# Moving preparation into the first projection, and splitting a normalised map by a threshold on the raw one

## Chip, core and metric

The kernel runs on one core of one Trainium2 chip. The metric is the device time of the program in microseconds (us), the median of several runs. A profile is one more execution, taken by the hardware profiler.

The engines are named as in the profile: PE (TensorE, matmuls; PEld its weight loads), DVE (VectorE), ACT (ScalarE), POOL (GpSimd) and SP (SyncE). SP computes nothing here: it issues nearly all DMA transfers, in one queue, in order. A `q` behind an engine's name means its sequencer, which waits or issues.

## What is computed

The input `x` is four images of 96 channels, 128 x 128. Two layers follow, each a residual around a group norm (32 groups of three channels).

```python
x = x + ssm(_gn(x))       # 1x1 to 192 channels, depthwise 3x3, silu, four scans
                          # (rows, columns, both directions), layer norm, 1x1 back to 96
x = x + attn(_gn(x))
```

The second layer subtracts the mean of the whole image, and splits the result into its positive part `x1` and its negative part `x2`. Each is normalised with statistics of its own (numbers of positives and negatives, sums, sums of squares):

```python
x1 = relu(x); x2 = x - x1
out = 0.5 * (nc1 * x1n + nc2 * x2n) + res_coef * x   # xr
half1, half2 = sc1 * x1 + x1n, sc2 * x2 + x2n
key, qry = conv3x3(half1, aw1), conv3x3(half2, aw2)  # attention over channels and taps
value = conv3x3(half1, aw3)                          # convolved with the attention's weights
y2 = layer_norm(conv3x3(half2, w_conv2)) * half1
result = xr + conv1x1([layer_norm(attended), y2], w_full) + b_full
```

## The kernel before

**Stages.** `image_stats(0)` takes the group norm's statistics of image 0 (32 chunks of 96 x 512, one `bn_stats` each). `project(b)` makes the 192 channels of image b: 16 strips of eight rows, in each a load of the strip (`strip_in`), the norm on ACT (L454), seven shifted copies by DMA (L462, L467), 56 matmuls (L611) into three rotating PSUM banks, tanh on ACT (L486) and its product on DVE (L487), then the small projections for the scan (`rows_out`, `cols_out`) and stores. `ssm_scan` is one long generator over 384 steps; each has two halves with a scan on DVE (L831), softplus and exponential on ACT, and products on POOL and DVE. `norm` of an image is `ssm_output` (layer norm and the 1x1, into `xnew` in DRAM) and then `split_norm`. `direct_maps` makes keys, queries and attention weights of image 0; `attend` those of the other images and, for all, the attended map `od`; `close` (`attn_output`) is the last stage and writes the output.

**Order.** The generators are woven by hand. `co_run(left, right, pace)` draws `left`, and for each unit of its declared cost as much of `right` as `pace` says. From project 0 to the end of `direct_maps(0)`, `in_order` fixes the order of emission on every engine and on SP's queue: an instruction that waits holds all that is emitted behind it on that engine. Projects 0, 1 and 2 with 3 run beside the scan at paces 0.25, 0.75 and 1.35; the scan cannot begin before eight strips of project 0 are there, and needs all of it for its second direction. After that `norm(0)` runs beside the scan at 0.5, `direct_maps(0)` at 0.95. In the second part, `attend(b)` runs beside `close(b-1)` and `norm(b+1)`; `close(3)` runs alone at the end. There the order is left to the compiler's scheduler.

**What the change touches.**

- `image_stats(b + 1)` runs beside `project(b)`: a generator `beside`, drawn four times a strip (L623, L633), which loads a chunk of 192 KB (L401, one buffer) and takes its `bn_stats` (L404) one draw later. `project` then makes mean and variance with `bn_aggr` in `combine` (L181) and two small matmuls (L183, L190).
- Behind project 3 come `new_map` (borders of the six padded maps x1d, x2d, vd of two sets: twelve DMAs, L1175 and L1176) and `pair_weights` (3x3 weights of the attention: twelve loads into `g`, L1202; sums and differences of taps on DVE, L1185 to L1189; four stores `wd`, L1211; two passes over one buffer). Then `ssm_output` of image 0 loads `y` (L927) and sums it on PE (L938).
- `split_norm` has two passes over `xnew`, each of 16 chunks of 96 x 1024. The first takes counts and sums with `scale=a, bias=shift0` inside the Relu. The second first normalises the chunk in place on ACT (L1150), then makes for each half `scale * x + shift` on ACT (L1156), and masks it by the sign of the normalised chunk on DVE (L1161). Loads are L1041, stores L1165; a memset on POOL (L1154) clears the border column.
- `attn_output` does the same for its 16 chunks: it loads o, c2 and xx (L1718), normalises `xx` in place on ACT (L1727), makes x1 (ACT L1731, mask L1732), `c2 = (c2 - mean) * x1` (L1733), `e` (ACT L1737, mask L1738, L1739), two matmuls a half (L1743, L1744) and the sum (L1745); each tile has two buffers.

Of the kernel before, what the change touches and what calls it, by code (L numbers as in the profile page):

```python
# [9 lines left out]
F32 = mybir.dt.float32  # L10
# [7 lines left out]
C = 96  # L18
# [44 lines left out]
def kernel(  # L63
# [86 lines left out]
    ones = filled(1.0, "ones")  # L150
# [25 lines left out]
    def combine(ps, stats, mat, name):  # L176


        n = stats.shape[0]
        mv = small.tile([n, 2], F32, name=f"mv{n}", tag=f"mv{n}")  # L180
        nc.vector.bn_aggr(mv, stats)  # L181
        p1 = bank(ps)[:n, 0:2]
        nc.tensor.matmul(p1, lhsT=mat, rhs=mv, start=True, stop=True)  # L183
        r = small.tile([n, 2], F32, name=name, tag=name)
        nc.vector.tensor_copy(r, p1)
        d2 = small.tile([n, 1], F32, name=f"d2{n}", tag=f"d2{n}")
        nc.vector.tensor_sub(d2, mv[:, 0:1], r[:, 0:1])
        nc.vector.tensor_mul(d2, d2, d2)
        p2 = bank(ps)[:n, 0:2]
        nc.tensor.matmul(p2[:, 0:1], lhsT=mat, rhs=d2, start=True, stop=True)  # L190
        nc.vector.tensor_add(r[:, 1:2], r[:, 1:2], p2[:, 0:1])
        return r, mv
# [150 lines left out]
    def project_weights(pool):  # L343

        ws = []
        with tc.tile_pool(name="wq", bufs=1, side="left") as pq:
            for k, parts in enumerate(STACK):
                n = (128, 128, C + KK + 1)[k]  # L350
                m = 3 if k < 2 else 1
                w = pool.tile([n, m, 2 * C], F32, name=f"wp{k}")
                raw = pq.tile([n, 2 * C], F32, name=f"raw{k}")
                for p, c0, c1, dh, d in parts:
                    q = p + c1 - c0
                    nc.sync.dma_start(raw[p:q], in_wT[c0:c1])
                    src = dw_wT[3 * dh : 3 * dh + 3] if k < 2 else dw_wT[6 + d : 7 + d]
                    nc.sync.dma_start(w[p:q], src.partition_broadcast(q - p))
                if k == 2:
                    nc.sync.dma_start(raw[C : C + KK], in_b[0].partition_broadcast(KK))  # L360
                    nc.sync.dma_start(w[C : C + KK, 0], dw_wT)
                    nc.gpsimd.dma_start(
                        w[n - 1 : n, 0].rearrange("p (j c) -> p j c", j=2),
                        dw_b.rearrange("c j -> j c").unsqueeze(0),
                    )
                    nc.sync.dma_start(
                        raw[n - 1 : n].rearrange("p (j c) -> p j c", j=2),
                        ones[0:1].unsqueeze(1).to_broadcast([1, 2, C]),
                    )
                nc.vector.tensor_scalar(raw, raw, 0.5, None, ALU.mult)  # L370
                nc.vector.tensor_mul(w, w, raw.unsqueeze(1).to_broadcast([n, m, 2 * C]))
                ws.append(w)

            one = pq.tile([128, PW], F32, name="one")
            nc.vector.memset(one, 1.0)
            nc.vector.memset(one[:, 0:1], 0.0)
            where = dram.tile([1, (H + 2) * PW + 4], F32, name="where", bufs=1)
            nc.sync.dma_start(where[:, 0:PW], zeros[0:1, 0:PW])
            nc.sync.dma_start(
                where[0, PW : (H + 1) * PW].rearrange("(h w) -> h w", w=PW), one  # L380
            )
            nc.sync.dma_start(where[:, (H + 1) * PW :], zeros[0:1])
            taps = dram.tile([KK + 1, H * PW], F32, name="taps", bufs=1)
            for t in range(KK):
                at = (t // 3) * PW + t % 3
                nc.sync.dma_start(taps[t : t + 1], where[:, at : at + H * PW])
            nc.vector.memset(one, 1.0)
            nc.sync.dma_start(taps[KK].rearrange("(h w) -> h w", w=PW), one)
        return ws, taps

    def image_stats(b, pool):

        stats = pool.tile([C, NCH, 6], F32, name=f"stats{b % 2}", tag=f"stats{b % 2}")

        def run(p2, ahead):
            xf = x[b].rearrange("c h w -> c (h w)")
            tiles = []
            for i in range(NCH + ahead - 1):
# [6 lines left out]
                yield 0.7  # L405

        return stats, run

    def project(b, weights, stats, beside, zb, xrows, ps):
# [10 lines left out]
        with tc.tile_pool(name="a2", bufs=2, side="left") as p2:  # L420
            beside = beside(p2, 1) if beside else iter(())
# [20 lines left out]
            gs, _ = combine(ps, stats.rearrange("p c s -> p (c s)"), gmean, "gs")  # L442
# [155 lines left out]
            for s in range(last + 1):  # L598
# [3 lines left out]
                for q in range(3):  # L602
                    pz = bank(ps)
                    for i, (k, d) in enumerate(terms):
# [17 lines left out]
                        if i == 4:  # L622
                            next(beside, None)  # L623
# [4 lines left out]
                    if q == 1:  # L628
# [4 lines left out]
                        next(beside, None)  # L633
# [398 lines left out]
    def split_norm(xnew, x1d, x2d, stats, keep, cnt, ps, side):  # L1032


        with tc.tile_pool(name="n2", bufs=2, side=side) as p2:
# [10 lines left out]
            gs, mv = combine(ps, stats.rearrange("p c s -> p (c s)"), gmean, "gs1")  # L1046
            a = col("rstd1")
# [7 lines left out]
            shift0 = col("b1")  # L1055
# [35 lines left out]
            nc.tensor.matmul(pt, lhsT=ones, rhs=c5, start=True, stop=True)  # L1091
            g5 = col("g5", 5)
            nc.vector.tensor_copy(g5, pt)
# [34 lines left out]

            rs, rh, half = col("rs", 2), col("rh", 2), col("half", 2)
# [4 lines left out]


# [3 lines left out]
            ia = col("ia")  # L1139
            nc.vector.reciprocal(ia, a)  # L1140
            nc.vector.tensor_add(low[:, 0:1], rs[:, 1:2], ia)
            nc.vector.tensor_add(low[:, 1:2], rh[:, 1:2], bful)
            nc.vector.tensor_mul(ia, ia, shift0)
            nc.vector.tensor_sub(low[:, 1:2], low[:, 1:2], ia)
            keep.update(up=up, low=low, a=a, b=shift0, scale=scale, shift=shift)

            for i in range(NS):
                y = ahead.pop(0)
                piece(i + 3)
                nc.scalar.activation(y, y, AF.Identity, scale=a, bias=shift0)  # L1150
                v = y.rearrange("p (h w) -> p h w", w=W)
                for side_, m in ((0, x1d), (1, x2d)):
# [9 lines left out]
                        to, v, 0.0, to, op, ALU.mult  # L1162
# [28 lines left out]
    def pair_weights():  # L1191


        four, nine = [], []
        with tc.tile_pool(name="wq", bufs=1, side="left") as pw:
            for i, pair in enumerate(((aw1, aw3), (aw2, w_conv2))):
                g = pw.tile([C, 3, 3, 2, C], F32, name="g")
                for j, src in enumerate(pair):
                    v = src.rearrange("c (h w) o -> c h w o", w=3)
                    for w in range(3):  # L1200

                        nc.sync.dma_start(g[:, :, w, j], v[:, :, w if j else 2 - w])  # L1202
                g = g.rearrange("p h w j o -> p h w (j o)")
# [9 lines left out]
        return four, nine  # L1213
# [450 lines left out]
    def attn_output(img, ps, side):  # L1664
        keep = img.keep
        up, low, scale, shift = (keep[n] for n in ("up", "low", "scale", "shift"))
        ob = out[img.b].rearrange("c h w -> c (h w)")
        with (
# [54 lines left out]
            for t in range(NS):  # L1723
                o, c2, xx = ahead
                if t + 1 < NS:
                    ahead = loads(t + 1)
                nc.scalar.activation(  # L1727
                    xx, xx, AF.Identity, scale=keep["a"], bias=keep["b"]
                )
                x1 = p3.tile([C, SN], F32, name="x1")  # L1730
                nc.scalar.activation(x1, xx, AF.Identity, scale=scale[:, 0:1], bias=shift[:, 0:1])  # L1731
                nc.vector.scalar_tensor_tensor(x1, xx, 0.0, x1, ALU.is_gt, ALU.mult)  # L1732
# [5 lines left out]
                nc.vector.scalar_tensor_tensor(e, xx, 0.0, e, ALU.is_gt, ALU.mult)  # L1738
# [55 lines left out]
    def projections(images, weights, stats, wp, ps):  # L1794
        for b in images:
            beside = None
            if b + 1 < NB:
                stats[b + 1], beside = image_stats(b + 1, wp)
# [8 lines left out]
    with tc.tile_pool(name="wp", bufs=1, side="left") as wp:  # L1807
# [7 lines left out]
        for images, pace in (([0], 0.25), ([1], 0.75), ([2, 3], 1.35)):  # L1815
            left = projections(images, weights, stats, wp, psl)
            if images[0] == 0:
                next(left)
                next(others)
                while ready[0] < 2:  # L1820
                    next(left)
                wdt, wbc, outws, outbs = next(others)
            co_run(left, last, pace)
            drain(left)
    maps = [
        [new_map(f"{n}{i}") for n in ("x1d", "x2d", "vd")] for i in range(2)
    ]
    four, nine = pair_weights()
# [113 lines left out]
```

## Time and profile before

| | |
|---|---|
| Median of 3 runs (lowest, highest) | 6966.72 us (6951.81, 6972.1) |
| The profiled execution | 6980.28 us |
| Its span, first to last instruction | 6978.5 us |
| Mean granted TensorE clock | 0.888 |
| First matmuls of projects 0, 1, 2, 3 | 56.3, 440.3, 899.1, 1526.8 us |
| `ssm_output` of image 0, first matmul | 2165.6 us |
| Second pass of `split_norm`, image 0 | 2500.6 to 2603 us |
| Scan, first to last | 304.1 to 3395.8 us |
| Last close, first `bn_aggr` to the end | 6849.0 to 6978.5 us |

Times in the profile are microseconds from the span's start unless marked ns. A row of busy time by stretches gives each engine's busy time and, behind x, its instructions. A row of waits gives what waited for what: the sum in us, the number of times, the longest. A row of the timeline gives start, duration, engine, line, operation, names, and in brackets the engine's idle time before it with what ended it. "A<-B" reads: A is written from B. Matmul ends are modelled, so busy PE is not PE at its peak.

### The profile page before, as it was taken

To read this page: it belongs to the slowest core of one execution; us is meant where nothing else is said; L and a number is where in the kernel's file an instruction comes from. 1 tells how busy PE (TensorE), PEld (TensorE's weight loads), DVE (VectorE), ACT (ScalarE), POOL (GpSimd) and SP (SyncE) were. 2 spreads that over 40 slices of the span, in tenths; PEclk is the share of its full clock that TensorE was granted. 3 is DMA by queue.
4 is the path that set the end of the run, shared out by engine and by line. 5 is a ranking of instruction groups with operands and counts; after the bars stand their busy time and mean duration, and the time that the engine had idled before them with its cause. 6 is when DMAs were issued, how large, how long until landed. Compare 5 with 4: busy or idle time off the path is not lost. (4 is left out here: it accounts for less than half of the span.)

```text
span 6978.5 us, 74317 instructions
## 1 busy us (share of the span) xinstructions
PE 5676.2 (81%) x22236; PEld 2332.2 (33%) x22236; DVE 4892.9 (70%) x6892; ACT 3065.2 (44%) x3813; POOL 3395.1 (49%) x2072
## 2 busy tenths in 40 slices
PE   6989978878885629999977488986788986788987
PEld 2323323222221104444422234442334342334432
DVE  3257779889895778888466675668765568775587
ACT  1357767777873486676312422223222124221113
POOL 2137669778792228778222243333433333444641
PEclk9999989989996659999988789997899998899998
DMA  6657777856755666766567765667665667565555
GB/s 143 156 144 190 198 206 203 231 162 179 209 169 166 188 190 193 206 182 174 165 182 188 202 162 147 177 168 206 167 161 146 166 167 204 166 175 140 134 156 170
DMA packets 798481, 1227.58 MB, mean 176 GB/s; under 512 B 217698, under 2 KB 557674, under 8 KB 785600
## 3 DMA queue, kind: packets, MB, share of 16 engines
q1 hardware_dynamic: 795184, 1222.45, 64.1%
q8 instruction: 178, 2.92, 0.2%
q14 instruction: 223, 1.83, 0.1%
q0 software_dynamic: 2896, 0.39, 0.1%
HBM read 858.12 MB, written 296.46 MB: 165 GB/s over the span
## 5 line engine op out<-in xcount | busy, mean ns | idle before, releaser
L1256 POOL TENSOR_TENSOR t<-y 128x768 f32<-128x768 f32 (+1 forms) x352 | 552.6, 1570 | 1929.2 <-DMA y<-vd 550.9
L611 PE MATMUL bank<-y,wp 128*128 128x512 f32 (+3 forms) x3584 | 1323.5, 626 | 80.1 <-DMA y<-y 34.7
L843 POOL TENSOR_TENSOR y<-y,dl 128x1024 f32<-128x1024 f32 x384 | 1051.3, 2738 | 569.6 <-DVE dl L835 533.6
L810 POOL TENSOR_TENSOR dl<-dl,u 128x1024 f32<-128x1024 f32 x384 | 1006.1, 2620 | 459.5 <-ACT dA L786 232.8
L1280 PE MATMUL bank<-t,wd 128*128 128x384 f32 (+2 forms) x4224 | 1137.8, 495 | 37.6 <-DVE s L1322 16.1
L831 DVE TENSOR_TENSOR_SCAN dA<-dA,pBC 128x512 f32<-128x512 f32 x768 | 981.5, 1278 | 30.8 <-DVE pBC L814 0.5
L1329 ACT COPY s<-bank 128x384 f32<-128x384 f32 (+2 forms) x292 | 136.0, 466 | 1934.1 <-PE bank L1291 1871.2
L835 DVE TENSOR_TENSOR dl<-dA,pBC 128x512 f32<-128x512 f32 x768 | 528.0, 688 | 317.8 <-PE pBC L724 251.2
L1280 PEld LDWEIGHTS bank<-t,wd 128*128 128x128 f32 (+1 forms) x4224 | 559.6, 170 | 565.0 <-issue 319.9
L1280 PE MATMUL bank<-t,wa 128*96 128x384 f32 (+1 forms) x1408 | 565.3, 550 | 206.7 <-DVE t L1257 140.1
L611 PEld LDWEIGHTS bank<-y,wp 128*128 128x128 f32 (+3 forms) x3584 | 460.5, 169 | 752.6 <-issue 664.8
L724 PE MATMUL pBC<-xr,wbc 60*128 60x512 bf16 (+1 forms) x1536 | 443.0, 404 | 300.0 <-DVE dA L831 240.8
L1638 PE MATMUL bank<-y,wn 128*128 128x384 f32 (+5 forms) x2408 | 654.2, 498 | 32.7 <-DMA y<-x1d 17.4
L1321 DVE TENSOR_TENSOR d<-s,bank 128x384 f32<-128x384 f32 (+2 forms) x292 | 156.2, 535 | 661.8 <-ACT s L1329 539.8
L653 ACT ACTIVATE dl<-pd,dtb 128x512 f32<-128x512 f32 x768 | 486.1, 684 | 186.8 <-PE pd L724 172.9
L814 DVE TENSOR_TENSOR pBC<-dl,pBC 128x512 f32<-128x512 f32 x768 | 527.0, 686 | 2.1 <-POOL dl L810 0.9
L786 ACT ACTIVATE dA<-dl,negA 128x1024 f32<-128x1024 f32 x384 | 420.3, 1142 | 2.3
L1280 PEld LDWEIGHTS bank<-t,wa 128*96 128x96 f32 x1408 | 241.8, 185 | 516.2 <-issue 288.2
L1638 PEld LDWEIGHTS bank<-y,wn 128*128 128x128 f32 (+3 forms) x2408 | 304.1, 166 | 302.9 <-issue 130.5
L1257 POOL TENSOR_TENSOR t<-y 128x384 f32<-128x384 f32 (+1 forms) x352 | 383.7, 1090 | 0.0
L1258 POOL TENSOR_TENSOR t<-y 128x384 f32<-128x384 f32 (+1 forms) x352 | 381.0, 1082 | 0.0
L653 ACT ACT_TABLE_LOAD x245 | 314.3, 1283 | 115.5 <-PE pd L724 112.4
(247 smaller groups left out, 7662.6 us busy)
## 6 DMA issues: line engine op xcount, KB each, us to landing
u<-zb SPq DMA_DIRECT2D x192, 1024.0 KB
yms<-y SPq DMA_DIRECT2D x96, 512.0 KB
y<-yms SPq DMA_DIRECT2D x64, 768.0 KB
xn<-xnew SPq DMA_DIRECT2D x128, 384.0 KB
y<-y SPq DMA_DIRECT2D x128, 258.2 KB
zb<-z SPq DMA_DIRECT2D x64, 512.0 KB
y<-vd SPq DMA_DIRECT2D x168, 193.8 KB
y<-in_x SPq DMA_DIRECT2D x56, 480.0 KB
```

Source lines behind the costliest of these rows:

```text
L611: nc.tensor.matmul(blocks(pz[p:e]), lhsT=ws[k][:, d, c : c + e - p], rhs=window(ys[k], at, d, n), start=(i == 0), stop=(i == len(terms) - 1),)
L653: nc.scalar.activation(dst, src, AF.Softplus, bias=bias)
L724: nc.tensor.matmul(p, lhsT=w[rows], rhs=xr[rows, at : at + CH], start=True, stop=True)
L786: nc.scalar.activation(live[m]["dA"], live[m]["dl"], AF.Exp, scale=negA[:, g % 3, k : k + 1])
L810: nc.gpsimd.tensor_mul(t, t, u_view(n))
L814: nc.vector.tensor_mul(p, live[n]["dl"][:, bass.ts(half, CH)], p)
L831: nc.vector.tensor_tensor_scan(h, h, p, init, ALU.mult, ALU.add)
L835: nc.vector.tensor_mul(live[n]["dl"][:, sl], live[n]["dA"][:, sl], live[n]["C", half])
L843: nc.gpsimd.tensor_add(v, v, t.rearrange("p (a b) -> p a b", b=W))
L1256: eng.tensor_sub(v[:, 0:2], of(y, 0), of(y, 2))
L1280: nc.tensor.matmul(pc[p:e, :n], lhsT=w[:, i, c : c + e - p], rhs=t[k][:, i, :n], start=(k == 0), stop=False,)
L1638: nc.tensor.matmul(pc[p:e, :n].rearrange("p (h w) -> p h w", w=W), lhsT=w[:, c : c + e - p], rhs=v[:, :, 0:W], start=(i == 0), stop=(i == ...
```

## The change

Statistics of images 1, 2 and 3 are all taken within project 0, one after the other, in two chunk buffers; `beside` is drawn twelve times a strip in place of four. Each generator ends with its own `bn_aggr` into a small tile that stays, and `combine` takes that. `pair_weights` becomes a generator: its loads (now two buffers, on the memory's other side) are issued behind the first matmuls of project 0, and the map borders and its arithmetic and stores follow when four strips are through. In `split_norm` the norm's scale `a` and shift `shift0` are folded into scale and shift of both halves and into the two pairs of the last stage, and a threshold `thr = -shift0 / a` per channel takes the place of 0.0 in the masks, so that L1150 and L1727 go. `ones` is a small tile of its own where it is needed; sums over channels use `mean96` times 96.

```diff
-    def combine(ps, stats, mat, name):
+    def combine(ps, stats, mat, name, mv=None):
...
-        n = stats.shape[0]
-        mv = small.tile([n, 2], F32, name=f"mv{n}", tag=f"mv{n}")
-        nc.vector.bn_aggr(mv, stats)
+        if mv is None:
+            mv = small.tile([stats.shape[0], 2], F32, name="mv", tag=f"mv{stats.shape[0]}")
+            nc.vector.bn_aggr(mv, stats)
+        n = mv.shape[0]
...
-        stats = pool.tile([C, NCH, 6], F32, name=f"stats{b % 2}", tag=f"stats{b % 2}")
+        stats = pool.tile([C, NCH, 6], F32, name="stats", tag="stats")
+        mv = const.tile([C, 2], F32, name=f"stats{b}", tag=f"stats{b}")
...
-        return stats, run
+            nc.vector.bn_aggr(mv, stats.rearrange("p c s -> p (c s)"))
+
+        return mv, run
...
-            beside = beside(p2, 1) if beside else iter(())
+            beside = chain(*(run(p2, 2) for run in beside))
...
-            gs, _ = combine(ps, stats.rearrange("p c s -> p (c s)"), gmean, "gs")
+            gs, _ = combine(ps, None, gmean, "gs", mv)
...
-                        if i == 4:
+                        if i in (2, 4, 6):
                             next(beside, None)
...
-                        next(beside, None)
+                        for _ in range(3):
+                            next(beside, None)
...
-            nc.vector.tensor_add(low[:, 0:1], rs[:, 1:2], ia)
+            nc.vector.tensor_copy(low[:, 0:1], rs[:, 1:2])
             nc.vector.tensor_add(low[:, 1:2], rh[:, 1:2], bful)
-            nc.vector.tensor_mul(ia, ia, shift0)
-            nc.vector.tensor_sub(low[:, 1:2], low[:, 1:2], ia)
-            keep.update(up=up, low=low, a=a, b=shift0, scale=scale, shift=shift)
+
+            for m, s in ((scale, shift), (up[:, 0:1], up[:, 1:2]), (low[:, 0:1], low[:, 1:2])):
+                nc.vector.scalar_tensor_tensor(s, m, shift0, s, ALU.mult, ALU.add)
+                nc.vector.tensor_scalar(m, m, a, None, ALU.mult)
+            nc.vector.tensor_scalar(low[:, 0:1], low[:, 0:1], 1.0, None, ALU.add)
+            thr = col("thr")
+            nc.vector.reciprocal(thr, a)
+            nc.vector.scalar_tensor_tensor(thr, shift0, -1.0, thr, ALU.mult, ALU.mult)
+            keep.update(up=up, low=low, thr=thr, scale=scale, shift=shift)
...
-                nc.scalar.activation(y, y, AF.Identity, scale=a, bias=shift0)
...
-                        to, v, 0.0, to, op, ALU.mult
+                        to, v, thr, to, op, ALU.mult
...
-        four, nine = [], []
-        with tc.tile_pool(name="wq", bufs=1, side="left") as pw:
-            for i, pair in enumerate(((aw1, aw3), (aw2, w_conv2))):
+        four, nine, taps = [], [], []
+        with tc.tile_pool(name="wq", bufs=2, side="right") as pw:
+            for pair in ((aw1, aw3), (aw2, w_conv2)):
...
+                taps.append(g)
+            yield
+            for i, g in enumerate(taps):
...
-        return four, nine
+        yield four, nine
...
-                nc.scalar.activation(
-                    xx, xx, AF.Identity, scale=keep["a"], bias=keep["b"]
-                )
                 x1 = p3.tile([C, SN], F32, name="x1")
...
-                nc.vector.scalar_tensor_tensor(x1, xx, 0.0, x1, ALU.is_gt, ALU.mult)
+                nc.vector.scalar_tensor_tensor(x1, xx, thr, x1, ALU.is_gt, ALU.mult)
...
-                nc.vector.scalar_tensor_tensor(e, xx, 0.0, e, ALU.is_gt, ALU.mult)
+                nc.vector.scalar_tensor_tensor(e, xx, thr, e, ALU.is_gt, ALU.mult)
...
-            beside = None
-            if b + 1 < NB:
-                stats[b + 1], beside = image_stats(b + 1, wp)
+            beside = []
+            for i in range(1, NB) if b == 0 else ():
+                stats[i], run = image_stats(i, wp)
+                beside.append(run)
...
                 next(left)
                 next(others)
+                made = pair_weights()
+                next(made)
                 while ready[0] < 2:
                     next(left)
+                maps = [
+                    [new_map(f"{n}{i}") for n in ("x1d", "x2d", "vd")] for i in range(2)
+                ]
+                four, nine = next(made)
                 wdt, wbc, outws, outbs = next(others)
...
-    maps = [
-        [new_map(f"{n}{i}") for n in ("x1d", "x2d", "vd")] for i in range(2)
-    ]
-    four, nine = pair_weights()
     istats = [ctx.enter_context(tc.tile_pool(name="istats0", bufs=1, side="left"))]
```

## The prediction, made before the changed kernel was run

> **What bounds the kernel now.** I read the page's first part, then busy time by stretches, then the timeline of the one stretch in which TensorE does nothing, then rows and waits of the edited lines.
>
> ```profile
> PE 5676.2 (81%) x22236; PEld 2332.2 (33%) x22236; DVE 4892.9 (70%) x6892; ACT 3065.2 (44%) x3813; POOL 3395.1 (49%) x2072
> ```
>
> No engine binds throughout: 81% is a mean over stages with different limits. The stretches, in order: strips of project 0, 1, 2 and 3; the passage behind project 3; the halves of image 0; those of image 1; the last close. Columns: PE, PEld, DVE, ACT, POOL busy, granted clock, DMA share, GB/s.
>
> ```profile
> core 0: us, PE busy (x) PEld busy (x) DVE busy (x) ACT busy (x) POOL busy (x), PEclk, DMA share, GB/s
> 56.00:324.00 268.00, 257.15 (x915) 95.91 (x915) 60.58 (x93) 76.41 (x104) 43.16 (x69) 0.99 0.60 145
> 440.30:840.30 400.00, 375.25 (x1402) 125.04 (x1402) 300.31 (x380) 292.08 (x334) 256.93 (x94) 0.97 0.69 184
> 899.10:1449.40 550.30, 473.04 (x1624) 160.29 (x1624) 489.97 (x603) 414.92 (x478) 430.44 (x168) 0.94 0.78 218
> 1526.80:2054.60 527.80, 463.05 (x1622) 143.98 (x1622) 469.64 (x569) 411.34 (x473) 448.19 (x167) 0.93 0.68 190
> 2119.40:2165.50 46.10, 1.54 (x4) 0.25 (x3) 12.14 (x16) 1.19 (x2) 7.35 (x4) 0.50 0.51 138
> 2503.00:2600.00 97.00, 17.98 (x34) 3.90 (x33) 78.00 (x68) 83.29 (x79) 25.83 (x40) 0.50 0.74 225
> 3866.00:3890.00 24.00, 0.00 (x0) 0.00 (x0) 15.05 (x15) 20.17 (x18) 1.08 (x10) 0.50 0.89 268
> 6875.00:6965.00 90.00, 60.24 (x94) 18.82 (x95) 71.05 (x70) 41.20 (x35) 0.00 (x0) 0.77 0.72 205
> ```
>
> Projects 0 and 1 are TensorE's (96%, 94%). In 2 and 3 the scan runs at full pace and VectorE carries 89%. In the passage nothing works. The timeline of it:
>
> ```profile
> 2116.66 3.33 SPq L571 DMA_DIRECT2D xrows<-cp  x6
> ...
> 2125.76 3.93 SPq L1202 DMA_DIRECT2D g<-in_aw  x6
> ...
> 2132.04 0.95 DVE L1185 COPY wt<-g 96x1152 f32<-96x1152 f32 x1 [11.95 <-DMA g<-in_aw]
> ...
> 2148.88 0.96 DVE L1185 COPY wt<-g 96x1152 f32<-96x1152 f32 x1 [13.27 <-DMA g<-in_w_conv]
> ...
> 2159.67 1.30 SPq L927 DMA_DIRECT2D y<-yms  x3
> ...
> 2165.57 1.89 PE L938 MATMUL bank<-y,mean 96*32 96x512 f32 x2 [44.41 <-DMA y<-yms]
> ```
>
> SyncE ends project 3's stores at 2120.0, issues twelve map borders, loads g, waits for VectorE and the stores (one buffer), loads g again, and only at 2159.67 loads image 0's y. VectorE stands in front of L1185, so the scan queued behind it stands too, and TensorE waits 44.41 us for y.
>
> **The passage (gain).** All of it moves. Without it the y loads follow the last cp store: 2159.67 - 2120.0 = 39.7 us. They may have to wait until that store has landed; at the end of project 0 the clearing of y0 waited until 430.9, 1.2 us behind the last issue's end (429.7). Everything behind (sums, scan, norm) is in emission order and follows y, so it comes earlier by the same. Next late there is y's own landing, 5.8 us. I take 38, ends 30 and 40.
>
> One rule speaks against expecting anything: the Trainium skill (Perfetto Trace Analysis, Identifying Performance Opportunities) says that improvement comes from the most-contended engine. That is PE, and the change takes no matmul away: by the rule the sum is 0. The row decides: PE is busy 1.54 of these 46.1 us, so this stretch is a chain of waits, worth its 38 us.
>
> **Statistics out of projects 1 and 2 (gain).** Each loses 32 loads of 192 KB and 32 L404. Projects 2 and 3 are nearly one experiment: equal strips, 167 and 165 scans (L831 in the two stretches), 30 L404 against none. 550.3 - 527.8 = 22.5 us; two scans at 527.8/165 = 3.2 us are 6.4 of that. So 16 to 22.5: 18. Project 1 is on TensorE at 94% with VectorE at 75%: its 20.5 us of L404 (30 x 0.683) lie beside matmuls. Ends 0 and 20.5, taken 3, near the PE-bound row.
>
> **Statistics into project 0 (cost).** 64 more L404, 43.7 us of VectorE (busy 60.6 of 268), and 12.6 MB over some 370 us: 34 GB/s on 145, below the 218 that project 2 moves. Hidden by TensorE's 96%, if VectorE's waits stay short:
>
> ```profile
> DVE stats L404 <- DMA xst<-in_x: 41.9, 12, 10.3
> ```
>
> Between 56 and 440 us, 12 of 32 chunks waited, 3.5 us each. Queued behind an L404 are L487 and the casts' subtractions that free TensorE's three banks; behind these waits, now three times as many, PE stands. In a strip of 21.4 us L487 ends 5 to 6 us before its bank is taken again (ends 209.3, 215.8; the next groups 214.3, 222.4), and today no PE wait on it is long. Distance from load to L404 stays alike: three calls of a third of the spacing, with two buffers. On SyncE six loads a strip, each waiting for the L404 two before, stand ahead of the shifts; the shifts end at 216.1 for matmuls at 229.6, 13 us of cover. I take 0 here.
>
> What does show: (a) twelve g loads (0.61 us each, 7.3 us of SyncE) ahead of strip 1's input; strip 1's shifts end at 69.6, matmuls start at 78.0 and a shift lands in 2.4 (437.8 to 440.1 at project 1's start): 6 us of cover, the g traffic beside it, so 3 us. (b) at strip 4 twelve borders (5 us of SyncE), 7.3 us of VectorE and four wd stores that SyncE can't issue before VectorE: 3 us. (c) 3 x 66 = 198 steps against 16 x 12 = 192 calls: three chunks are drained behind the cp stores (SyncE 429.7); landing near 435, L404, bn_aggr and the 3.5 us of combine put L454 at 440 instead of 436.4: 4 us. (d) 1 us elsewhere. Sum 11; ends -2 and 35.
>
> **Borders, ones, mean96, combine without bn_aggr.** A few 0.1 to 1.0 us instructions, in project starts that wait for y<-in_x anyway (436.2, when shift had been ready since 424.2): 0; without that cover bn_aggr's 1.0 us a project.
>
> **Halves from xnew (gain).** L1150, 16 per image at 1.24 us, goes; L1161 gets a pointer in place of 0.0. VectorE's price for that is shown by neighbours of the same shape (min/median/max in ns):
>
> ```profile
> L1738 DVE SCALAR_TENSOR_TENSOR e<-xx,e x64: 1209/1215/2494, 3969.8 to 6970.1; 96x1024 f32<-96x1024 f32 x64
> L1739 DVE SCALAR_TENSOR_TENSOR e<-xx,low,e x64: 1267/1276/2493, 3974.0 to 6971.4; 96x1024 f32<-96x1024 f32 x64
> ```
>
> 0.06 us each, 1.9 us for 32. Image 0: ScalarE is busy 83.3 of 97 us, so it bounds there; 16 x 1.24 = 19.8 go, but VectorE (78) and the two-buffer loop memset, ScalarE, VectorE, store, landing come next: 10, ends 0 and 19. Image 1 alone (3866 on): 268 GB/s at a DMA share of 0.89, so the loads and stores bound it: 4, ends 0 and 10. Images 2 and 3 run beside convolutions where VectorE is late; it waits 23.3 us for L1156 in all of 3964:6840: 6, ends -3 and 20.
>
> **Closes from xnew (gain).** L1727 (64 x 1.24) leaves the chain load, L1727, L1731, L1732, L1733, matmul; TensorE stands at its end between 3964 and 6840:
>
> ```profile
> PE bank L1744 <- DVE c L1733: 44.3, 21, 3.9
> ```
>
> 21 waits x 1.24 = 26 at most; much of it returns as a later wait in a stage at 90% PE: 12, ends 0 and 26. Last close: 7 us a step with two buffers; a step of VectorE is 1.22 + 1.27 + 1.21 + 1.28 + 2 x 0.74 = 6.46, plus 0.12 for the pointers. 1.24 per two steps over 14 steps is 8.7; with the floor 16 x 6.58 = 105 of 112 us: 5, ends 0 and 9.
>
> **Sum.** -38 - 18 - 3 + 11 - 10 - 4 - 6 - 12 - 5 = -85 us. The profiled execution took 6980.3 (span 6978.5 and 1.8 around it), 13.6 above the median 6966.7; 85 is taken off the median: 6882.
>
> **Rivals.**
> Only the passage counts: work removed beside other work is worth nothing, as TensorE's 94% in project 1 suggests and the 22.5 us between projects 2 and 3 deny. 6966.7 - 38 + 11 = 6940. Chance 0.17.
> Relief reaches further: every removed ScalarE instruction shortens a chain of the attention, all gains near their upper ends (40 + 22 + 10 + 16 + 7 + 15 + 22 + 7 = 139, less 11): 6839. For it: VectorE's 46.9 us of waits for L1731; against it: ScalarE is 44% busy. Chance 0.12.
> It does not do what it says: y stays held by project 3's stores or buffers and 30 of the passage's 38 us come back: 6912. Chance 0.04.
> Slower: VectorE's waits in project 0. If the cover of L487 is used up and each of 96 chunks costs PE half of the 3.5 us, 168 us stand against 96 of gains: 7039. It decides from 1.0 us a chunk on, strips of 27 us in place of 21.4. Against it: no such PE wait today. Chance 0.04.
> The likeliest: 0.63, between 6850 and 6915.
>
> **Range and chances.** 6840 to 6935: all of the likeliest, the fourth mechanism's return, half of the far relief and half of the passage alone; left out are about 0.18. Faster by over 0.3% (21 us, about what a measurement of this kernel can tell from no change), below 6946: 0.63 + 0.12 + 0.04 and 0.12 of the first rival: 0.91. The rest of that rival 0.05 same, 0.04 slower.
>
> **What would show it.** Right: the first L927 some 2 us behind the last L571; L1185 on g near 150 us; strips of project 2 like those of project 3 (35.2 us); strips of project 0 still near 21.4; halves of image 0 at 5.6 us in place of 6.3 (97 us, 31 L1161). Wrong: PE waiting on L487 or on y<-y within project 0; a wait of L927 on zb or xrows; project 2's strips at 36.7 as before.

## The result and the profile after

The changed kernel takes 6916.8 us (median of four runs, 6908.1 to 6921.7) against 6959.9 before on the same chip: ratio 0.9935, 95% interval 0.9915 to 0.9956, that is 31 to 59 us less, 45 by the ratio. 85 were forecast. The time lies in the forecast range and on its side; nearly half of the gain is missing.

Page line of the changed kernel:

```profile
PE 5662.7 (82%) x22236; PEld 2330.5 (34%) x22236; DVE 4920.7 (71%) x6916; ACT 2913.8 (42%) x3685; POOL 3397.6 (49%) x2072
```

VectorE has 28 us more, ScalarE 151 us less (the affine of halves and closes). Now the stretches of the changed kernel, with the columns and the order of the prediction's table; project 0 is cut here from the first matmul of strip 0 to that of strip 15, and the first fence is that stretch before.

```profile
56.30:390.20 333.90, 322.78 (x1161) 119.83 (x1161) 90.07 (x132) 106.77 (x141) 58.93 (x77) 0.99 0.61 149
```

```profile
57.20:436.20 379.00, 336.49 (x1162) 124.38 (x1162) 133.75 (x202) 106.17 (x143) 59.68 (x77) 0.94 0.70 175
492.80:881.80 389.00, 375.38 (x1402) 125.16 (x1402) 282.77 (x350) 291.64 (x333) 256.74 (x94) 0.97 0.67 176
939.80:1464.60 524.80, 468.51 (x1625) 161.32 (x1625) 472.72 (x573) 414.86 (x478) 429.77 (x168) 0.95 0.78 217
1537.60:2060.30 522.70, 459.20 (x1622) 142.75 (x1622) 469.59 (x569) 411.41 (x473) 448.42 (x167) 0.93 0.69 192
2119.40:2131.30 11.90, 3.25 (x9) 0.52 (x6) 9.04 (x11) 4.76 (x6) 10.35 (x5) 0.50 0.77 154
```

Project 0 takes 379.0 in place of 333.9 us for the same matmuls. Of these 45.1 us, 13.7 are TensorE's own busy time (336.49 for 322.78): the granted clock is 0.94 in place of 0.99. The rest is TensorE standing. Project 1 (389.0 for 400.0) and project 2 (524.8 for 550.3) are shorter, and project 2 is now project 3's equal, as said. The passage, from the timeline of the changed kernel:

```profile
2117.54 6.60 SPq L572 DMA_DIRECT2D xrows<-cp  x12
2125.56 1.31 SPq L929 DMA_DIRECT2D y<-yms  x3
...
2131.34 1.89 PE L940 MATMUL bank<-y,mean 96*32 96x512 f32 x2 [6.01 <-DMA y<-yms]
```

The y loads follow the last cp store by 1.4 us, and TensorE waits 6.01 in place of 44.41 us. From the end of project 3's last projection matmul (L612) to this one it is 40.0 us; it was 78.5.

The waits of project 0 (57 to 493 us), where the prediction had 12 waits of L404 and no long one of TensorE on L487:

```profile
DVE stats L404 <- DMA xst<-in_x: 209.3, 43, 18.6
ACT y L455 <- DMA y<-in_x: 105.5, 13, 17.9
PE bank L612 <- DVE z L488: 21.7, 5, 6.5
```

So the sign that the prediction named as "wrong" is there. (L612 is the projection's matmul and L488 what frees its bank, L487 before.)

SyncE waits too. A chunk load at L401 waits until its buffer is free, and what stands behind it in SyncE's order waits with it. SyncE's own waits at L401 in project 0, before (56 to 440 us) and in the changed kernel (57 to 493 us):

```profile
SPq L401 <- DVE stats L404: 16.4, 6, 9.2
SPq L401 <- DMA xst<-in_x: 2.1, 1, 2.1
```

```profile
SPq L401 <- DMA xst<-in_x: 42.6, 18, 6.3
SPq L401 <- DVE stats L404: 24.5, 30, 7.9
```

That is 67.1 us in place of 18.5. Issuing its 96 chunks takes SyncE another 52.4 us there (13.1 for 32 before).

### The profile page after: what moved, and what is told of

It reads as the page before. It is cut to its first block, busy times and chain, and to the rows that moved or that the text cites. A ratio compares the mean times of both kernels' runs of the same rounds, so it can differ in the third digit from the quotient of the medians.

```text
span 6917.3 us, 74304 instructions
## 1 busy us (share of the span) xinstructions
PE 5662.7 (82%) x22236; PEld 2330.5 (34%) x22236; DVE 4920.7 (71%) x6916; ACT 2913.8 (42%) x3685; POOL 3397.6 (49%) x2072
## 5 line engine op out<-in xcount | busy, mean ns | idle before, releaser
L612 PE MATMUL bank<-y,wp 128*128 128x512 f32 (+3 forms) x3584 | 1331.6, 632 | 69.1 <-DVE z L488 26.3
L1288 PE MATMUL bank<-t,wd 128*128 128x384 f32 (+2 forms) x4224 | 1120.2, 491 | 34.4 <-ACT s L1337 15.0
L612 PEld LDWEIGHTS bank<-y,wp 128*128 128x128 f32 (+3 forms) x3584 | 463.8, 171 | 749.1 <-issue 661.9
## 6 DMA issues: line engine op xcount, KB each, us to landing
xn<-xnew SPq DMA_DIRECT2D x128, 384.0 KB
```

The lines of the kernel that those rows point to most:

```text
L612: nc.tensor.matmul(blocks(pz[p:e]), lhsT=ws[k][:, d, c : c + e - p], rhs=window(ys[k], at, d, n), start=(i == 0), stop=(i == len(terms) - 1),)
L1288: nc.tensor.matmul(pc[p:e, :n], lhsT=w[:, i, c : c + e - p], rhs=t[k][:, i, :n], start=(k == 0), stop=False,)
```

## The experiments

Strips of project 0, from the start of a strip's first matmul to that of the next, in us, summed as marked; "end" is from strip 15 to project 1; the last column is the median against that of before measured beside it on the same chip, with the ratio's interval. All twelve runs are in it. Where medians and ratio differ, both are given below.

| kernel | strip 0 | 1-3 | 4 | 5-8 | 9-14 | end | median - before; ratio |
|---|---|---|---|---|---|---|---|
| before | 21.7 | 64.2 | 23.0 | 85.6 | 139.2 | 50.1 | |
| changed | 25.9 | 62.9 | 41.9 | 84.4 | 163.8 | 56.6 | -43; 0.9915-0.9956 |
| e1_stats | 22.4 | 62.4 | 23.0 | 83.2 | 161.6 | 56.5 | -18; 0.9961-0.998 |
| e2_prep | 22.8 | 64.2 | 34.3 | 85.6 | 139.0 | 50.7 | -25; 0.9954-0.998 |
| e3_thr | 21.6 | 64.2 | 23.0 | 85.6 | 139.5 | 50.0 | -14; 0.9973-0.999 |
| e4_fixed | 23.2 | 62.4 | 40.0 | 83.2 | 160.9 | 52.6 | -53; 0.9906-0.9933 |
| e5_pool | 25.6 | 62.4 | 61.1 | 83.2 | 142.4 | 50.8 | -64; 0.9895-0.9924 |
| e6_spread | 22.2 | 76.3 | 23.4 | 83.2 | 163.5 | 56.6 | -67; 0.9895-0.9923 |
| e7_both | 25.3 | 62.4 | 52.7 | 83.2 | 143.6 | 50.8 | -75; 0.9883-0.9913 |
| e8_noload | 22.5 | 62.4 | 33.2 | 83.2 | 138.8 | 50.7 | -92; 0.9856-0.9889 |
| e10_prepq | 24.2 | 62.4 | 28.5 | 84.6 | 164.1 | 56.5 | -59; 0.9886-0.9918 |
| e9_mix | 22.9 | 62.4 | 28.8 | 96.5 | 142.2 | 51.1 | -72; 0.9864-0.9897 |
| e11_late | 24.2 | 62.4 | 28.1 | 83.8 | 142.2 | 50.6 | -96; 0.9856-0.989 |
| e12_nothr | 25.8 | 62.4 | 42.0 | 84.8 | 161.0 | 56.6 | -41; 0.9919-0.9959 |

Strips are steady from run to run (21.4 or 20.8 where nothing collides, in every profile). Stages behind project 0 are not: where nothing was edited, a stage of 400 to 800 us differs by up to some 10 us between two profiles, and 35 runs of the kernel before lie between 6946.5 and 6978.7. So project 0 is read from profiles, and the whole from the timed runs; a single stage behind project 0 is not read from one profile.

The theory that I started from, T: L404 waits for its chunk on VectorE and so keeps L488 from freeing TensorE's bank. It is what the three waits above suggest.

**e1_stats, e2_prep, e3_thr: one part alone.** e1 takes the hunks of `image_stats`, `combine`, `project`, `projections` (and of the constant `ones`, for room); e2 those of `pair_weights` and its calls; e3 those of the halves and of `attn_output`. Their cores, one after the other:

```
-            beside = beside(p2, 1) if beside else iter(())
+            beside = chain(*(run(p2, 2) for run in beside))
...
+                made = pair_weights()
+                next(made)
                 while ready[0] < 2:
                     next(left)
+                maps = [
...
+                four, nine = next(made)
...
-                nc.scalar.activation(y, y, AF.Identity, scale=a, bias=shift0)
...
-                        to, v, 0.0, to, op, ALU.mult
+                        to, v, thr, to, op, ALU.mult
```

> Only the statistics of images 1 to 3 move into project 0; the preparation stays in the passage behind project 3 and the halves and closes keep their affine. Theory T (an L404 that waits for its chunk stands in front of the instruction that frees TensorE's bank): project 0 about +30 us (strips 9 to 13 about +23, its end about +6), project 1 about -11, projects 2 and 3 about -35 together, passage and attention unchanged; about -10 to -15 us in all. As the prediction had it (L404's waits hidden, only the drain costs): +5 in project 0 and -21 behind, -16. Rival S (project 0's loss is the preparation's pile alone): project 0 below +12, in all -30 or more.

> Only the map borders and the attention's weights move into project 0; statistics and threshold stay as before. The passage gives -38 us. Theory T: the first strip loses about 4 us and strip 4 10 to 19 us (borders, products and 3 MB of stores in one place, and L404 behind them), so -15 to -24 us in all. As the prediction had it (3 us at each place): -32. If strip 4 loses its 19 us only together with the tripled chunk loads, this run shows strip 4 below +8 and -30 or more in all.

> Only the threshold: halves and closes straight from xnew; projects and passage as before. From the stages of the changed kernel: halves of image 0 -4, attention stages -24 to -28 together, last close -4: -30 us, ends -24 and -36. As the prediction had it: -37 (10 + 4 + 6 + 12 + 5). If the attention's gain in the changed kernel comes from somewhere else (an earlier start, another order), this run gives less than -15.

By the ratios they give -21, -23 and -12: -56 together, and the whole change 45. Within the intervals they add up, and the strips show what is lost when they meet: strip 4 grows by 0 with the statistics, by 11.3 with the preparation, by 18.9 with both; strip 0 by 0.7, 1.1 and 4.2. Strips 9 to 14 are the statistics' alone (+22.4), and so is the end (+6.4). Rival S (the preparation's pile only) is out: e1's project 0 is 25.2 us longer (409.2 for 384.0), near T's 30 and far from the prediction's 5. In all e1 gives a little more than T said. The passage is the preparation's alone: 40.0 us in e2. The threshold alone missed its expectation, -12 in place of -30; less than -15 was named there as the sign that the attention's gain in the changed kernel comes from elsewhere.

**e4_fixed: L404 never waits.** The loads stay, but L404 reads a resident weight tile, so it leaves out the true statistics of images 1 to 3.

```
-    nc.vector.bn_stats(stats[:, i - ahead + 1], tiles.pop(0))
+    t = tiles.pop(0)
+    nc.vector.bn_stats(stats[:, i - ahead + 1], t if fixed is None else fixed)
```

> The changed kernel, with all 96 chunk loads kept, but L404 reads a resident weight tile in place of the chunk (so the statistics of images 1 to 3 are those of that tile): VectorE does the same work and never waits for a chunk. Theory T: L404's waits fall from 209 us to near 0 and project 0 becomes 25 to 40 us shorter than in the changed kernel, strip 4 part of it; in all -85 to -100 us against before. Rival R (SyncE's queue and the traffic of 12.6 MB more delay y and the shifts themselves): project 0 stays within 10 us of the changed kernel's, in all -55 to -70.

No wait of L404 on a load is left, and yet strips 9 to 14 (160.9) and strip 4 (40.0) hardly move; the end gives 4.0 us, strip 0 2.7. Project 0 is 13.5 us shorter than in the changed kernel, where T asked 25 to 40 and its rival less than 10; the total, -53 by the medians and -56 by the ratio, is nearest to the rival's. So T explains at most a quarter of the 51.6 us that project 0 had grown by, and next to nothing in strips 4 and 9 to 14. Another wait takes its place at once. Timeline of this kernel in strip 10, SyncE's issues and then TensorE:

```profile
271.84 8.29 SPq L574 DMA_DIRECT2D xrows<-cp  x12
...
285.51 3.41 SPq L401 DMA_DIRECT2D xst<-in_x  x3
...
295.90 2.09 SPq L716 DMA_DIRECT2D xr<-xrows  x6
```

```profile
298.60 0.58 PE L728 MATMUL pd<-xr,wdt 60*128 60x512 bf16 x1 [9.61 <-DMA xr<-xrows]
```

From 268 to 299 us one issue follows the other on SyncE: the row and cp stores of half an image, the strip's shifts, zb stores, and from 271 on six chunk loads. These take 5.1 us of it (0.56 + 0.46 + 3.41 + 0.69): 2.8 us of issuing and, within the 3.41, 2.2 us of waiting until an older chunk has landed in the same buffer. Over project 0 (57 to 480 us) this wait is

```profile
SPq L401 <- DMA xst<-in_x: 44.6, 20, 5.8
```

so e4 frees L404, but not SyncE. The scan's xr is issued at 295.9, and the scan's first matmul, in TensorE's order ahead of the projection, waits 9.61 us for it. What is late is SyncE's list, whichever instruction is found waiting.

**e5_pool: the same loads on another engine's queue.** Theory Q, from e4: SyncE's queue; rival D: the traffic.

```
-    nc.sync.dma_start(tiles[-1], xf[:, bass.ts(i, CH)])
+    queue.dma_start(tiles[-1], xf[:, bass.ts(i, CH)])     (queue = nc.gpsimd in project 0)
```

> The changed kernel with one word other: within project 0 the 96 chunk loads are issued by GpSimd in place of SyncE. Bytes, L404 and its waits for landing are as in the changed kernel. Theory Q (SyncE's queue: some 1 us of it for each chunk load, in strips that already hold twelve cp stores and the scan's loads, makes shifts and xr late): strips 9 to 14, 163.8 us in the changed kernel and 139.2 before, fall to 140 to 148, and all comes to -60 to -70 us against before. Theory D (the traffic itself): they stay at 158 or more, -40 to -48 in all. Strip 4 stays near 40 by both. If L404's wait were the cause after all, nothing moves either, but PE's waits keep L404 or L488 as their releaser.

Q holds: strips 9 to 14 fall from 163.8 to 142.4, and the end from 56.6 to 50.8, with the same bytes. What the traffic costs is at most the 3.6 us between 142.4 and e8's 138.8. Two things leave SyncE's list with the loads: their issues (18.3 us in the changed kernel's strips 9 to 14, 5.2 before) and their waits until an older chunk has landed and been read (25.9 us, 9.3 before). Which of them weighs more stays open: a kernel with more chunk buffers, all loads still on SyncE, was not run. The waits themselves go on, on GpSimd (first line below), where in strips 9 to 14 they delay nothing that shows. But strip 4 goes to 61.1, which I had not expected. GpSimd issues the 54 copies into wdt there (0.55 us each, with waits between), and the chunk loads queue behind them. The waits of this kernel (57 to 500 us), then VectorE, and GpSimd:

```profile
POOL xst L401 <- DVE stats L404: 271.4, 73, 17.7
PE bank L612 <- DVE z L488: 33.5, 3, 31.1
```

```profile
193.94 1.28 DVE L404 BATCH_NORM_STATS2 stats<-xst 96x6 f32<-96x512 f32 x2 [40.95 <-DMA xst<-in_x]
```

```profile
189.97 1.08 POOL L249 DMA_DIRECT2D wbc<-one  x2
191.04 1.07 POOL L401 DMA_DIRECT2D xst<-in_x  x2
```

Here T's mechanism does work: an L404 that waits 41 us for its chunk keeps TensorE's bank for 31 of them. So T is a real danger, but not what strips 9 to 14 of the changed kernel paid for.

**e6_spread: the preparation in pieces.** Six draws with strips between (g loads late in strip 0, products and stores late in strips 1, 2 and 3) in place of two:

```
+    for n in (5, 10, 3, 8, 3):
+        for _ in range(n):
+            next(left)
+        next(made)
+    for _ in range(8):
+        next(left)
+    four, nine = next(made)
```

> The changed kernel with the preparation spread over strips 0 to 3: g loads late in strip 0, products and the four stores of 3 MB one at a time late in strips 1, 2 and 3, after each strip's shifts; map borders late in strip 3. The same instructions, only elsewhere. If strip 4's pile (borders 5.5 us and stores 5 us of SyncE ahead of the strip's input, and the input's data behind 3 MB) is the cause of +19 there, strip 4 falls from 41.9 to 23 to 26 and strip 0 from 25.9 to 21 to 22, strips 1 to 3 grow by 0 to 2 each: 18 to 22 us better than the changed kernel, -63 to -67 against before. If each store costs wherever it lies, strips 1 to 3 take most of it back: under 8 us better.

Between the two: strip 4 falls to 23.4 and strip 0 to 22.2 as expected, but strips 1 to 3 take back 13.4. Strips 0 to 4 are 121.9 against 130.7: 8.8 better. (In all it is 24 us better than the changed kernel by the medians, 18 by the ratios, more than the 10 of project 0; strips decide here.) Beside the chunk loads the stores cost wherever they lie; a pile makes it worse.

**e7_both: both at once.** The two diffs above in one kernel.

> Both at once: chunk loads on GpSimd's queue and the preparation spread. If the two causes are separate, project 0 comes to within 10 us of its time before and all gains stay: -80 to -92 us against before. If they share one cause (SyncE's queue), the sum of the two single gains is not reached: -68 to -78.

Strips 1 to 3 and strip 4 are 62.4 and 52.7 here, not 76.3 and 23.4 as in e6. With the chunk loads gone from SyncE, the same stores at the same places cost nothing in strips 1 to 3, so what e6 lost there came from both in one queue. But with chunk loads waiting behind wdt's copies on GpSimd, strip 4 is lost again. -75 by the medians, -71 by the ratio (-60 to -82), is the number of the second expectation, but not its reason: strips 9 to 14 and the end are where e5 has them, and what is missing is lost in strip 4's collision.

**e8_noload: what the loads cost in all.** e4, and without the loads:

```
-    nc.sync.dma_start(tiles[-1], xf[:, bass.ts(i, CH)])
+    if fixed is None:
+        nc.sync.dma_start(tiles[-1], xf[:, bass.ts(i, CH)])
```

> The changed kernel without the 96 chunk loads: L404 reads a resident weight tile (so the statistics of images 1 to 3 are those of that tile), VectorE's work is the same. It bounds what the loads cost, by queue and by traffic together: strips 9 to 14 at 139 to 143 us as before, strip 4 at 34 as with the preparation alone, project 0 some 28 to 34 us shorter than in the changed kernel: -73 to -80 us against before. If strips 9 to 14 stay above 155, neither queue nor traffic is the cause and the 43.7 us of L404 on VectorE are.

Strips 9 to 14 are as before (138.8), although VectorE does all 64 L404 more. So VectorE's 43.7 us cost nothing there, as predicted; the loads cost it all. Strip 4 keeps 10.2 us of the preparation. In all -92 (by the ratio -89, -77 to -100), more than expected.

**e10_prepq: the preparation's transfers on GpSimd.** Borders, g loads and wd stores, at the same places; as the stores, so the others:

```
-    nc.sync.dma_start(wd, t)
+    nc.gpsimd.dma_start(wd, t)
```

> The changed kernel with the preparation's transfers (twelve g loads, twelve borders, four stores of 3 MB) issued by GpSimd at the same places; chunk loads stay on SyncE. If strips 0 and 4 lose by what stands on SyncE ahead of the next strip's input (7 us of g loads; 11 us of borders and stores), strip 0 falls from 25.9 to 21 to 22.5 and strip 4 from 41.9 to 25 to 30; strips 9 to 14 stay at 160 to 164; in all -58 to -66 us against before. If the 3 MB themselves hold the strip's input up on whatever queue, strip 4 stays above 35 and all above -56. GpSimd's list for wdt stands behind the stores then; the scan needs wdt only from strip 10 on, so nothing is taken for that.

Strip 4 falls by 13.4 to 28.5, so what stood ahead of the strip's input on SyncE was the larger part; the 3 MB are still moved. Strip 0 keeps 2.5 us, more than expected. In all -59 by the medians, -68 by the ratio, about as expected.

**e9_mix, e11_late: putting it together.** Both are e10 with another queue for some chunk loads; the first line below is e9's, the second e11's.

```
+    queue = nc.gpsimd if b > 1 else nc.sync
+    queue = nc.gpsimd if (b, i) >= (2, 12) else nc.sync
```

> As the one before, and the chunk loads of images 2 and 3 on GpSimd too, while those of image 1 (drawn in strips 0 to 5, where GpSimd works through wdt's list) stay on SyncE. From the single runs: strips 0 and 4 as in the one before, strips 9 to 14 at 142 to 145 as with all loads on GpSimd, the passage from project 0 to 1 within 1 us of before. Project 0 within 10 us of its time before, -82 to -95 us against before in all; the best of these kernels that computes the reference. If GpSimd's list collides again, strip 5 or 6 shows a wait of L404 above 10 us, and all stays above -75.

> As the last one, but GpSimd issues the chunk loads only from image 2's chunk 12 on (strip 7.5), behind wdt's list, which ended at 198 us there. Strip 5, 32.0 us with the chunk loads behind that list, falls to 21 to 23, strip 6 to 21; strips 9 to 14 stay at 142 to 145. Against before -85 to -95 us, some 10 better than the last one. If another strip takes the 11 us over (SyncE's queue in strips 5 to 7 carries the loads again), the total stays within 4 us of the last one's.

e9 shows the collision again, one strip on: 32.0 us in strip 5, L404 waiting 14.3. In all -72 by the medians, -83 by the ratio (-72 to -95), at the weak end of what was expected. e11 keeps the chunk loads off GpSimd until wdt's list is through: strip 5 is 21.4 again, strips 9 to 14 stay at 142.2. Its project 0:

```profile
56.90:397.60 340.70, 327.17 (x1162) 121.94 (x1162) 133.53 (x202) 106.61 (x141) 86.37 (x137) 0.98 0.75 192
```

6861.2 us against 6956.9, ratio 0.9873 (0.9856 to 0.989), 77 to 100 us less: the fastest kernel of this study that computes the reference, and faster than both given ones. It moves more per us than the changed kernel (192 for 175 GB/s) and yet is 38 us shorter in this stretch. Its project 0 is 12.6 us shorter than e9's; in the timed runs the two differ by less than their intervals.

**e12_nothr: the change without the threshold.** The changed kernel with e3's lines put back:

```
+                nc.scalar.activation(y, y, AF.Identity, scale=a, bias=shift0)
...
-                        to, v, thr, to, op, ALU.mult
+                        to, v, 0.0, to, op, ALU.mult
```

> The changed kernel with the threshold undone: halves and closes with their affine again, the rest as in the changed kernel. From the last direct convolution of image 0 to the end the profiles show 3506.8 us before, 3500.2 with the threshold alone and 3479.0 with the whole change. If these 28 us are the threshold's and only the profile of the threshold alone was a long one, this stretch is back at 3500 to 3507 and the total is -22 to -32 us against before. If most of them come with the other two parts (another placement of buffers and transfers), the stretch stays at 3478 to 3490 and the total is -35 to -42.

The ratio is 0.9939 beside 0.9935 of the whole change: by the timed runs the threshold cannot be seen within the change (-3, with intervals of 20 to either side), where alone it gave -12. The stretch from the last matmul of image 0's direct convolutions (L1638) to the end is 3482.8 us here and 3484.1 in the changed kernel. It is 3511.5 before, and 3509.0, 3509.9 and 3505.9 in e1, e2 and e3; the ten kernels that move both statistics and preparation lie between 3461 and 3487. (The expectation cut this stretch about 5 us later.) So some 20 to 25 us there go with moving both, with threshold or without. e12's halves and closes are those of before, so the threshold is not the reason; what is stays open.

## Why the prediction came out as it did

**The passage: right.** -38.5 measured, -38 said, by the mechanism that it named, and the rule of the most-contended engine was rightly set aside.

**Statistics out of projects 1 and 2: right for 2, too small for 1.** The strips lose 11.0 and 25.5 us in the changed profile. Taken over all profiles, the eleven kernels without these statistics have project 1's strips at 379.0 to 389.4 us (median 380.7) and the three with them at 396.0 to 403.3; project 2's are at 520.8 to 534.4 (527.6) and 544.3 to 550.4. So some 19 and 22 us stand against 3 and 18. The 3 was taken "near the PE-bound row", but TensorE was not bound throughout: the trace of before hid among shorter waits 13.7 us of TensorE on ScalarE's cast L575, of which 0.6 are left. The same wait of 0.57 us a strip is gone in project 0 (21.4 to 20.8). Which order of the two engines frees the bank sooner was not tried.

**Statistics and preparation into project 0: the step that failed.** The term was +11 and measures +52.5, outside its end of 35: strip 0 +4.2 for 3; strip 4 +18.9 for 3; the end +6.5 for 4; strips 9 to 14 +24.6, for which nothing was taken; the strips between -2.5, and a start 0.9 later. The arithmetic of L404 beside L487 ("I take 0 here") was mostly about the wrong engine: e8 shows that L404's work costs nothing, e4 that its waits cost 13.5 us, and e5 that the loads' places on SyncE's list cost 21.4 in strips 9 to 14. The prediction had the list at hand, "six loads a strip, each waiting for the L404 two before", and judged it by the shifts' cover of 13 us in an ordinary strip. In strips 9 to 14 that cover is used already: before, SyncE issues for 18 of strip 9's 21.5 us, with the cp stores and the scan's first loads in it, and strip 10 took 29.8. There each of 36 chunk loads puts its issue, 0.5 us in the mean, and its wait for a buffer, 0.7 us in the mean, ahead of all that stands behind it.

Strip 4 was mis-sized in the same way. Its timeline in the changed kernel, in order of time:

```profile
156.54 0.96 PE L263 MATMUL pw<-outws,mean 96*96 96x96 f32 x4 [7.46 <-DVE outws L251]
157.29 10.84 PE L612 MATMUL bank<-y,wp 128*128 128x512 f32 x22
160.79 2.45 SPq L437 DMA_DIRECT2D y<-in_x  x1
173.85 1.46 ACT L455 ACTIVATE y<-y,shift,rstd 96x1280 f32<-96x1280 f32 x1 [16.19 <-DMA y<-in_x]
174.19 1.28 DVE L404 BATCH_NORM_STATS2 stats<-xst 96x6 f32<-96x512 f32 x2 [15.12 <-DMA xst<-in_x]
176.56 3.68 PE L612 MATMUL bank<-y,wp 128*64 128x512 f32 x8 [6.47 <-DVE z L488]
```

Three things, where the prediction had one sum of 3 us. The products' 7.3 us stand on VectorE ahead of L251, and TensorE waits 7.46 for the scan's weights, an instruction in its order that the prediction did not list (0.62 before). The strip's input is issued at 160.8, behind borders and stores, and ScalarE gets it 13 us later, behind 3 MB. The tanh that L488 needs stands behind L455 on ScalarE, L404's chunk comes just as late, and TensorE waits 6.47 for L488; in e4, without L404's wait, it waits 9.35 at the same place. And TensorE runs slower after each stop. Windows of 4 us in the same strip, with the columns of the stretches above (the granted clock stands before the last two figures):

```profile
150.00:154.00 4.00, 0.00 (x0) 0.00 (x0) 3.93 (x7) 0.00 (x0) 0.00 (x0) 0.86 0.38 96
154.00:158.00 4.00, 1.46 (x5) 1.14 (x6) 2.30 (x7) 2.15 (x3) 2.16 (x4) 0.50 0.68 178
158.00:162.00 4.00, 4.00 (x9) 1.66 (x8) 1.08 (x2) 0.00 (x0) 2.75 (x6) 0.79 0.99 287
162.00:166.00 4.00, 4.00 (x11) 1.84 (x10) 0.00 (x0) 0.00 (x0) 0.80 (x2) 1.00 0.95 287
```

TensorE stops at 149.1. The clock is 0.50 from about 152.9 on (a mean of 0.86 in the first window is 1.1 us at 0.50), 3.8 us later. TensorE starts at 156.5, and the clock is full at about 159.7 (a mean of 0.79 is 1.7 us at 0.50), 3.1 us later. So a stop is paid for twice. The Trainium skill (TensorE: Matmul & The Clock Gate, What's actually happening) gives about 3.4 us of idleness until the clock falls to half and as much busy time until it is back; these rows agree within half a microsecond. Over project 0 the lower clock goes with 13.7 us of longer matmuls.

**Threshold: mis-sized too.** Halves and closes were put at -10, -4, -6, -12 and -5, together -37; alone it gives -12 (-7 to -19), within the change less than can be told. The halves of image 0, from the first to the last on ScalarE, lose 3.7 us (3.9 in e3; in e12, with the affine back, they take 0.3 more than before): the 19.8 us of ScalarE lay beside the loop of store and buffer, in which GpSimd's memset of the half waits 46.7 us for the store of x1d (61.4 before). The halves of image 1, on the DMA queues, lose nothing, and those of images 2 and 3 nothing either (+3.1 and +4.3). In the closes TensorE waits as before, with a step the less in the chain (3920 to 6790 us, changed kernel):

```profile
PE bank L1749 <- DVE c L1738: 51.6, 24, 3.5
```

It was 44.3 in 21 waits. "Much of it returns as a later wait" was too mild: by this row all of it does. The last close, from its `bn_aggr` to the end, is 125.7 us in place of 129.5, but that is no gain of the threshold: with the affine, e1, e2 and e12 take 126.4, 124.7 and 124.0. The pointer's price was right: L1737 takes 1.280 us at the median.

**The sum.** Up to image 0's first matmul behind the scan the changed profile is 34.2 us ahead; from image 0's direct convolutions to the end it gains another 27.4. (Together this is more than the timed 45, as the profile of before lies 20 us above the median of its runs.) The prediction, too, had 27 for that last stretch (4 + 6 + 12 + 5), all from the threshold. That they agree is luck: e12 has the same gain without the threshold, and e3, with the threshold alone, gains 5.6 there. Of the large misses, project 0 lost 41 us more than said, the threshold gave some 25 less, and project 1 gained up to 16 more. By an estimate from these profiles, without the unexplained 20 to 25 us the time would have been 6937 to 6942, outside the range, which ends at 6935; so the range held in part by luck.

The first rival says 6940, 23 us too slow. Its reason, that nothing is gained where work beside other work goes, is right for the threshold and wrong for the statistics. The rival that ends slower had its price from L404's waits; the true price comes mostly from SyncE's list, and e1's 25.2 us over 96 chunks are 0.26 us each, a quarter of its point of decision.

## What to carry to other kernels

Work moved under a busy engine is paid for on the queue that carries its transfers: count every issue that the moved step adds to SyncE, and every wait for a buffer that it brings into that list, strip by strip, and hold them against the strip in which that queue is fullest, not against an ordinary one. When a wait disappears and the time stays (e4), the named releaser was only the last of several late ones; ask what list they all stand in. Before putting transfers on an idle engine's queue, look for a long list that this engine gets elsewhere (e5: +19 us in one strip), and go round it (e11: 77 to 100 us less in all).

## What the runs showed that was not expected

- The Trainium skill (DMA: Bandwidth & Descriptors, Issuing engine by pattern) gives simple loads to Sync and calls that path generally faster. One issue does take longer on GpSimd here (0.51 us for a chunk load, 0.37 on SyncE in the same strips), and the load is still better placed there: 21.4 us in strips 9 to 14, because on SyncE what stands behind it is late.
- A chunk load or the strip's input, issued in 0.3 to 0.4 us elsewhere, takes SyncE longer right behind 3 MB of stores (strip 4: the last two stores 1.54 and 2.46, the input 2.45 us).
- The 43.7 us of statistics on VectorE, at 27% busy before, cost nothing that can be measured in strips 9 to 14 (e8).
- Two moves that meet in one strip cost more than the sum of both: strip 4 grows by 0, 11.3 and 18.9 us (e1, e2, the whole change).
- The stretch behind image 0's direct convolutions is some 20 us or more shorter in all ten kernels that move both other parts (above), in e12 too, whose halves and closes are those of before; the cause is open.
